# The last product of the position bias, one group of keys later

## The chip, the cores and the metric

The kernel runs on one NeuronCore of a Trainium2 chip. The time is the device time of one execution in microseconds; before the change it is 3762.87 us, the median of three runs (3762.15 to 3767.35). The profile is that of one more execution, with a span of 3758.9 us.

The engines have these names in it: PE is TensorE (matmul), PEld its weight load, DVE VectorE, ACT ScalarE, POOL GpSimd, SP SyncE.

## The reference

The network has four layers on x of shape (2, 512, 32, 32) in float32. The change is in layer 0, an attention with deformed keys: 8 heads and 2 images give 16 units (u in the kernel), each with 1024 queries and 64 keys. To each score a bias is added, that a small perceptron computes from the position of the query relative to the key:

```python
pos = grid_q[:, :, None, :] - grid_kv[:, None, :, :]
bias = jnp.sign(pos) * jnp.log1p(jnp.abs(pos))
bias = jax.nn.relu(bias @ cpb_w1 + cpb_b1)          # 2 -> 128
bias = jax.nn.relu(bias @ cpb_w2 + cpb_b2)          # 128 -> 128
bias = (bias @ cpb_w3 + cpb_b3).reshape(b, GROUPS, H * W, Hd * Wd)   # 128 -> 1
sim = jnp.einsum('bhid,bhjd->bhij', qh, kh) + bias
attn = jax.nn.softmax(sim, axis=-1)
```

That is done for 16 x 1024 x 64 pairs of query and key. The layer's own perceptron and layers 1 to 3 follow.

## The kernel before

A quad (u, o, jj) is a set of four keys of unit u; two of them (jj = 0 and 1) make a group (u, o), and there are 256 quads in 128 groups. For each quad VectorE makes the first hidden layer (line 390), one 128 x 1024 tile for each key. TensorE multiplies it with the second weights, 32 of the 128 outputs at a time (line 413). So there are four products q = 0 to 3 for a quad, each with the four keys side by side on the partitions. ScalarE applies the relu. The four results, each with its sign (flip), are added to one tile. Two of the three additions are made by transfers that add into their destination. The last of the three, `join`, is issued during the next quad, behind that quad's own first one.

```python
def second_hidden(self, u, o, jj, h1):
    nc = self.nc
    ys = []
    for q in range(4):
        hp = self.ps_h.tile([P, N], F32, tag="ps", ...)
        for h in range(2):
            cut = slice(h * HF, (h + 1) * HF)
            for k in range(4):
                rows = slice(32 * k, 32 * k + 32)
                nc.tensor.matmul(                                            # line 413
                    hp[rows, cut], lhsT=self.l0w2[:, 32 * q : 32 * q + 32], rhs=h1[k][:, cut], start=True, stop=True
                )
        y = self.hid2.tile([P, N], F32, tag=f"h2{q}", bufs=(2, 3, 2, 4)[q], ...)
        ys.append(y)
        nc.scalar.activation(y, hp, AF.Relu, bias=self.magb[:, q : q + 1])   # line 418
        if q == 1:
            nc.scalar.activation(ys[0], ys[0], AF.Copy, scale=self.flip[:, 0:1])               # line 420
            if jj == 1:
                nc.gpsimd.tensor_scalar(y, y, self.flip[:, 1:2], 1.0, ALU.mult, ALU.mult)      # line 422
            else:
                nc.scalar.activation(y, y, AF.Copy, scale=self.flip[:, 1:2])                   # line 424
            nc.gpsimd.dma_start(y, ys[0], accum_op=ALU.add)                  # line 425
            if self.join:
                self.join()
        elif q == 2:
            nc.gpsimd.tensor_scalar(y, y, self.flip[:, 2:3], 1.0, ALU.mult, ALU.mult)          # line 429
        elif q == 3:
            nc.gpsimd.tensor_tensor(y, y, ys[2], ALU.add)                    # line 431
    self.join = lambda: nc.gpsimd.dma_start(ys[3], ys[1], accum_op=ALU.add)  # line 432
    return ys[3]
```

The last product (line 445) multiplies the summed tiles z of the two quads of a group with one column per key, and so adds each key's bias to its row of the scores:

```python
def last_product(self, u, o, z, sims, ps_s):
    if o == 0:
        sims[u] = ps_s.tile([P, HF], F32, tag="sim", ...)      # one buffer
    for h in range(2):
        for jj in range(2):
            at = h * NJ + jj * 32
            nc.tensor.matmul(                                  # line 445
                sims[u][at : at + 32, :], lhsT=self.ends[:, 28 - 4 * o : 60 - 4 * o],
                rhs=z[jj][:, h * HF : (h + 1) * HF], start=(o == 0), stop=False,
            )
```

The loop over the quads has its order of instructions fixed for TensorE, ScalarE, VectorE and GpSimd. The first hidden layer is made one quad ahead. `offsets` and `sampled` (front: positions and sampled keys of the next pair of heads) and `attend` (after: the query-key product of line 460 on top of the bias, softmax, values) are cut into steps, and every quad takes one step of each.

```python
held, self.join = None, None
for i, (u, o, jj) in enumerate(quads):
    if o == 0 and jj == 0 and u % 2 == 0 and u // 2 + 1 < BP:
        nxt = pairs[u // 2 + 1]
        front += [self.offsets(nxt, ...), self.sampled(nxt, ...)]
    h1 = ready
    if i + 1 < len(quads):
        # (cut: before o = 7, front is driven on until the next pair's logarithms are there)
        ready = self.first_hidden(*quads[i + 1], pairs, tables)              # VectorE, line 390
    z = self.second_hidden(u, o, jj, h1)
    if jj == 0:
        first = z
    else:
        if held is not None:
            self.last_product(*held, sims, ps_s)
            if held[1] == 7:
                # (cut)
                after.append(self.attend(v, pairs[v // 2], sims.pop(v), att, ps))
        held = (u, o, (first, z))
    self.step(after)
    self.step(front)
self.join()
self.last_product(*held, sims, ps_s)
after.append(self.attend(u, pairs[u // 2], sims.pop(u), att, ps))
```

Of `offsets` the steps matter that put long work on VectorE: six products of a 6 x 6 window (line 243, three to a step) and their sum (line 256). Its first step sets the border of a padded tile to zero on GpSimd (line 232); that tile has two buffers, and `attend` reads the other pair's.

Of the kernel before, what the change touches and what calls it, by code (L numbers as in the profile page):

```python
# [11 lines left out]
F32 = mybir.dt.float32  # L12
AF = mybir.ActivationFunctionType
ALU = mybir.AluOpType
# [4 lines left out]
P = 128  # L19
B, C, H, W = 2, 512, 32, 32  # L20
N = H * W
# [5 lines left out]
BP = B * CT  # L27
# [20 lines left out]
class Net:  # L48
# [50 lines left out]
    def layer0(self):  # L99


        nc, io = self.nc, self.io
        with ExitStack() as ctx:
            keep = self.pool(ctx, "l0")
            self.l0qkv = keep.tile([P, 3, CT, P], F32, tag="qkv", name="qkv")
            nc.scalar.dma_start(self.l0qkv, io["l0_qkv"])
            self.l0w2 = keep.tile([P, P], F32, tag="w2", name="w2")
            nc.scalar.dma_start(self.l0w2, io["cpb_w2"])
            ow = keep.tile([P, CT, C], F32, tag="ow", name="ow")
            nc.scalar.dma_start(ow, io["out_w"])  # L110
            self.s1 = self.bn(keep, "bn1")
            self.last_weights(keep)

            self.dram = ctx.enter_context(self.tc.tile_pool(name="l0_d", bufs=2, space=bass.MemoryType.DRAM))
            self.fpool = self.pool(ctx, "f", 2)
            self.fone = self.pool(ctx, "f1", 1)
            self.lpool = self.pool(ctx, "c_log", 2)
            self.tab = self.pool(ctx, "c_tab", 2)
            self.hid = self.pool(ctx, "c_hid", 4)
            self.hid2 = self.pool(ctx, "c_hid2", 1)  # L120
            self.soft = self.pool(ctx, "c_soft", 1)
            apool = self.pool(ctx, "c_att", 1)
            ps = self.ps_h = self.pool(ctx, "c_ps_h", 3, psum=True)

            self.bank = self.pool(ctx, "c_ps_t", 1, psum=True).tile([P, HF], F32, tag="bank", name="bank")
            ps_s = self.pool(ctx, "c_ps_s", 1, psum=True)

            engines = {getattr(mybir.EngineType, e) for e in ("PE", "Activation", "DVE", "Pool")}
            with self.tc.manual_schedule(engines=engines):
                pairs = [{} for _ in range(BP)]  # L130
                for _ in self.offsets(pairs[0], 0, ps):
                    pass
                front = [self.sampled(pairs[0], 0, ps)]
                after, sims, att = [], {}, None
                tables = {}
                quads = [(u, o, jj) for u in range(2 * BP) for o in range(8) for jj in range(2)]
                ready = self.first_hidden(*quads[0], pairs, tables)
                held, self.join = None, None
                for i, (u, o, jj) in enumerate(quads):
                    if o == 0 and jj == 0 and u % 2 == 0 and u // 2 + 1 < BP:  # L140
                        nxt = pairs[u // 2 + 1]
                        front += [self.offsets(nxt, u // 2 + 1, ps), self.sampled(nxt, u // 2 + 1, ps)]
                    h1 = ready
                    if i + 1 < len(quads):
                        if quads[i + 1][1:] == (7, 0) and u + 1 < 2 * BP:
                            self.advance(front, lambda: "logs" in pairs[(u + 1) // 2])
                        ready = self.first_hidden(*quads[i + 1], pairs, tables)
                    z = self.second_hidden(u, o, jj, h1)
                    if jj == 0:
                        first = z  # L150
                    else:
                        if held is not None:
                            self.last_product(*held, sims, ps_s)
                            if held[1] == 7:
                                v = held[0]
                                if v % 8 == 0:
                                    self.advance(after, lambda: False)
                                    att = [
                                        apool.tile([P, N], F32, tag=f"att{t}", name=f"att{v}_{t}") for t in range(CT)
                                    ]  # L160
                                self.advance(front, lambda: "v" in pairs[v // 2])
                                after.append(self.attend(v, pairs[v // 2], sims.pop(v), att, ps))
                                if v % 8 == 7:
                                    after.append(self.projection(ps, att, ow, v // 8))
                        held = (u, o, (first, z))
                    self.step(after)
                    self.step(front)
                self.join()
                self.last_product(*held, sims, ps_s)
                after.append(self.attend(u, pairs[u // 2], sims.pop(u), att, ps))  # L170
                self.advance(after, lambda: False)
                self.project(ps, att, ow, "out_b", B - 1)
# [225 lines left out]
                h1.append(h[:, k, :, :].rearrange("p y x -> p (y x)"))  # L398
        return h1

    def second_hidden(self, u, o, jj, h1):

        nc = self.nc
        ys = []
        for q in range(4):
            hp = self.ps_h.tile([P, N], F32, tag="ps", name=f"hp_{u}_{o}{jj}{q}")
            for h in range(2):
# [3 lines that stand above are left out]
                    nc.tensor.matmul(  # L413
                        hp[rows, cut], lhsT=self.l0w2[:, 32 * q : 32 * q + 32], rhs=h1[k][:, cut], start=True, stop=True
                    )
            y = self.hid2.tile([P, N], F32, tag=f"h2{q}", bufs=(2, 3, 2, 4)[q], name=f"h2_{u}_{o}{jj}{q}")
            ys.append(y)
            nc.scalar.activation(y, hp, AF.Relu, bias=self.magb[:, q : q + 1])  # L418
            if q == 1:
                nc.scalar.activation(ys[0], ys[0], AF.Copy, scale=self.flip[:, 0:1])  # L420
                if jj == 1:
                    nc.gpsimd.tensor_scalar(y, y, self.flip[:, 1:2], 1.0, ALU.mult, ALU.mult)  # L422
                else:
                    nc.scalar.activation(y, y, AF.Copy, scale=self.flip[:, 1:2])  # L424
                nc.gpsimd.dma_start(y, ys[0], accum_op=ALU.add)  # L425
                if self.join:
                    self.join()
            elif q == 2:
                nc.gpsimd.tensor_scalar(y, y, self.flip[:, 2:3], 1.0, ALU.mult, ALU.mult)  # L429
            elif q == 3:  # L430
                nc.gpsimd.tensor_tensor(y, y, ys[2], ALU.add)  # L431
        self.join = lambda: nc.gpsimd.dma_start(ys[3], ys[1], accum_op=ALU.add)  # L432
        return ys[3]

    def last_product(self, u, o, z, sims, ps_s):
# [720 lines left out]
```

## Time and profile before

| | |
|---|---|
| Time, median of three runs | 3762.87 us |
| Layer 0 in the span | up to about 2260 us |
| Line 413, second hidden layer, TensorE | 1891.9 us in 16384 matmuls |
| Line 390, first hidden layer, VectorE | 1180.9 us in 1024 |
| Line 418, relu, ScalarE | 1120.3 us in 1024 |
| Line 431, addition, GpSimd | 614.8 us in 256, 2402 ns each |
| Line 429, sign, GpSimd | 448.8 us in 256 |
| Lines 425 and 432, adding transfers | 512 issues, 512 KB each, 6.5 us from issue to landing at the median |

A group of instructions on the page is given by line, engine and operation, with its busy time, the mean of one instruction, and the time for which its engine sat idle before it, with what ended that idle time. Two readings need care. A 32-column matmul of this kernel is listed with 593 ns, but four of them run side by side, so the listed times overlap. And a transfer's instruction on GpSimd covers only its issue; its end is the landing, which stands by itself. "Idle" of an engine that is not the bottleneck costs nothing.

### The profile page before, as it was taken

The numbers are of one execution on the slowest core, as the hardware profiler recorded it, in microseconds if no ns is written. First come the engines' busy times: TensorE is split into PE (matmuls) and PEld (weight loads), VectorE is DVE, ScalarE is ACT, GpSimd is POOL, SyncE is SP. The second block draws the span as 40 slices with busy tenths as digits, with TensorE's granted clock in tenths as the row PEclk, the third lists the DMA queues.
The fourth block names the chain that finished last, engine by engine and source line by source line (L and its number), as shares of the span: only waits on it lengthen the run. The fifth ranks groups of instructions, "written<-read, shape, count | busy, mean of one in ns | idle before, by whom it ended". The sixth has DMA issues, their size and how long they took to land.

```text
span 3758.9 us, 58788 instructions
## 1 busy us (share of the span) xinstructions
PE 3579.0 (95%) x25152; PEld 1393.5 (37%) x25152; DVE 2055.7 (55%) x2070; ACT 1972.0 (52%) x2001; POOL 1864.5 (50%) x1397
## 2 busy tenths in 40 slices
PE   5999999999999999999999989999989999999999
PEld 2333333333333333333333434444464333343333
DVE  5777766767766567767766641000052376522773
ACT  4776776777776576776777761000110266211661
POOL 3776776776776576776777760000001244012441
PEclk9999999999999999999999999999999999999999
DMA  5776776776776576776777762000000000000001
GB/s 143 142 139 135 142 147 126 148 143 133 142 150 127 113 146 123 145 147 129 158 145 148 153 139 114 0 0 0 0 3 0 34 1 1 16 0 1 1 1 46
DMA packets 102356, 336.77 MB, mean 90 GB/s; under 512 B 12608, under 2 KB 14272, under 8 KB 100800
## 3 DMA queue, kind: packets, MB, share of 16 engines
q0 software_dynamic: 73728, 268.47, 37.8%
q1 hardware_dynamic: 27488, 62.34, 5.5%
q8 instruction: 201, 3.29, 0.3%
q10 hardware_dynamic: 864, 2.06, 0.1%
q14 instruction: 75, 0.61, 0.1%
HBM read 59.92 MB, written 4.46 MB: 17 GB/s over the span
## 4 chain that ended last, share of the span: by engine, by line
PE 57%; POOL 15%; issue 12%; DMA 7%; DVE 6%; ACT 3%; POOLq 0%; ACTq 0%; SPq 0%; DVEq 0%
PE hp L413 15%; DMA h<-h 6%; POOL h L431 6%; PE m L549 6%; PE m L558 6%; PE s L886 6%; PE o L915 6%; PE pb L515 3%; PE qk0p L778 3%; PE qk1p L778 3%; POOL h L425 3%; PE vp L819 3%; POOL h L432 2%; ACT h L418 2%; DVE h L390 2%
## 5 line engine op out<-in xcount | busy, mean ns | idle before, releaser
L413 PE MATMUL hp<-h,w 128*32 128x512 f32 x16384 | 1891.9, 593 | 25.5 <-DVE h L390 18.1
L418 ACT ACTIVATE h<-hp,magb 128x1024 f32<-128x1024 f32 x1024 | 1120.3, 1111 | 586.3 <-PE hp L413 586.3
L390 DVE CUSTOM_DVE_ANT_1 h<-tx,bank 128x1024 f32<-128x1024 f32 x1024 | 1180.9, 1216 | 360.7 <-PE hp L413 352.3
L413 PEld LDWEIGHTS hp<-h,w 128*32 128x32 f32 x16384 | 668.8, 110 | 1130.6 <-issue 905.9
L431 POOL TENSOR_TENSOR h<-h,h 128x1024 f32<-128x1024 f32 x256 | 614.8, 2402 | 21.4
L425 POOL DMA_DIRECT2D h<-h x256 | 225.0, 879 | 547.6 <-ACT h L424 493.3
L429 POOL TENSOR_SCALAR h<-h,flip 128x1024 f32<-128x1024 f32 x256 | 448.8, 1753 | 0.0
L890 ACT ACTIVATE e<-s 128x1024 f32<-128x1024 f32 x256 | 258.6, 1023 | 152.9 <-PE s L886 152.7
L445 PE MATMUL sim<-h,ends 128*32 128x512 f32 x1024 | 229.2, 603 | 82.7 <-DMA h<-h 82.5
L432 POOL DMA_DIRECT2D h<-h x256 | 299.7, 1171 | 1.6 <-issue 1.3
L420 ACT ACTIVATE h<-h,flip 128x1024 f32<-128x1024 f32 x256 | 291.2, 1137 | 0.0
L886 PE MATMUL s<-q,k 64*64 64x512 f32 x2048 | 259.9, 590 | 5.4 <-ACT e L890 3.7
L915 PE MATMUL o<-e,v 64*64 64x512 f32 x2048 | 260.8, 592 | 0.0
L589 POOL MEMSET l1ones<- 128x128 f32 x1 | 0.2, 198 | 487.2 <-PE m L558 487.2
L549 PE MATMUL m<-mx,w 128*128 128x512 f32 x512 | 220.5, 592 | 0.9 <-issue 0.9
L553 ACT ACTIVATE mh<-m,cols 128x512 f32<-128x512 f32 x64 | 44.0, 687 | 336.5 <-PE m L549 336.5
L558 PE MATMUL m<-mh,w 128*128 128x512 f32 x512 | 220.4, 592 | 0.0
L897 POOL TENSOR_TENSOR some<-some,e 128x1024 f32<-128x1024 f32 x64 | 151.2, 2363 | 82.7 <-ACT e L890 80.3
L566 DVE SCALAR_TENSOR_TENSOR x<-m,cols,x 128x512 f32<-128x512 f32 x16 | 12.0, 751 | 318.0 <-PE m L558 318.0
L895 POOL TENSOR_TENSOR some<-e,e 128x1024 f32<-128x1024 f32 x32 | 75.7, 2367 | 212.9 <-ACT q L924 139.2
L792 POOL TENSOR_TENSOR sq<-q 128x1024 f32<-128x1024 f32 x16 | 30.3, 1893 | 280.1 <-DVE q L786 280.1
L422 POOL TENSOR_SCALAR h<-h,flip 128x1024 f32<-128x1024 f32 x128 | 152.3, 1190 | 30.6 <-ACT h L418 30.6
(184 smaller groups left out, 2796.2 us busy)
## 6 DMA issues: line engine op xcount, KB each, us to landing
h<-h POOLq DMA_DIRECT2D x512, 512.0 KB, 6.5
lb<-logs SPq DMA_DIRECT2D x64, 512.0 KB, 5.1
w<-in_mlp_w SPq DMA_DIRECT2D x8, 1024.0 KB, 11.9
qkv<-in_l_qkv SPq DMA_DIRECT2D x8, 768.0 KB, 6.5
x<-in_x SPq DMA_DIRECT2D x8, 512.0 KB, 7.9
out<-x SPq DMA_DIRECT2D x8, 512.0 KB, 2.6
proj<-in_l_proj SPq DMA_DIRECT2D x8, 256.0 KB, 5.9
l1w<-in_l_w SPq DMA_DIRECT2D x1, 1280.0 KB, 8.0
```

The source lines that it names most:

```text
L390: self.nc.vector._custom_dve(TENSOR_ADD_SAT, out=h[:, k, :, :], in0=x[:, jj, 2 * r + k, :].unsqueeze(1).to_broadcast([P, H, W]), in1=y[:, ...
L413: nc.tensor.matmul(hp[rows, cut], lhsT=self.l0w2[:, 32 * q : 32 * q + 32], rhs=h1[k][:, cut], start=True, stop=True)
L418: nc.scalar.activation(y, hp, AF.Relu, bias=self.magb[:, q : q + 1])
L420: nc.scalar.activation(ys[0], ys[0], AF.Copy, scale=self.flip[:, 0:1])
L425: nc.gpsimd.dma_start(y, ys[0], accum_op=ALU.add)
L429: nc.gpsimd.tensor_scalar(y, y, self.flip[:, 2:3], 1.0, ALU.mult, ALU.mult)
L431: nc.gpsimd.tensor_tensor(y, y, ys[2], ALU.add)
L432: self.join = lambda: nc.gpsimd.dma_start(ys[3], ys[1], accum_op=ALU.add)
L549: nc.tensor.matmul(acc, lhsT=w1[t][:, o * P : (o + 1) * P], rhs=xn[t], start=(t == 0), stop=(t == CT - 1))
L558: nc.tensor.matmul(acc, lhsT=w2[t // 4][:, t % 4, o * P : (o + 1) * P], rhs=hs[t], start=(t == 0), stop=(t == nh - 1),)
L886: nc.tensor.matmul(s[halves[c], par, :], lhsT=ks[p][rows, at : at + DH], rhs=qs[p][rows, cut], start=True, stop=True)
L915: nc.tensor.matmul(o[halves[par], r, :], lhsT=v[rows, n, at : at + DH], rhs=e[rows, par, :], start=(n == 0), stop=(n == NB - 1),)
```

## The change

The last product of a group is issued a quad later: behind the matmuls of the first quad (jj = 0) of the second group after it, where before it stood behind the second quad (jj = 1) of the first group after it. The adding transfer of the group's second quad so has one more quad of four keys in which to land. Up to two finished groups are held, and the tiles z get a fifth buffer. `attend`, which follows a unit's last product, moves along, and the front of the next pair of heads starts three quads later (o = 1, jj = 1), behind it. In the final quad the additions that were transfers, and the one of GpSimd, are made on VectorE, as nothing is left there to hide a transfer.

```diff
-                held, self.join = None, None
+                held, self.join = [], None
                 for i, (u, o, jj) in enumerate(quads):
-                    if o == 0 and jj == 0 and u % 2 == 0 and u // 2 + 1 < BP:
+                    if o == 1 and jj == 1 and u % 2 == 0 and u // 2 + 1 < BP:
...
-                    z = self.second_hidden(u, o, jj, h1)
-                    if jj == 0:
+                    z = self.second_hidden(u, o, jj, h1, i + 1 == len(quads))
+                    if jj == 1:
+                        held.append((u, o, (first, z)))
+                    else:
                         first = z
-                    else:
-                        if held is not None:
-                            self.last_product(*held, sims, ps_s)
-                            if held[1] == 7:
-                                v = held[0]
+                        if len(held) == 2:
+                            v, last, zs = held.pop(0)
+                            self.last_product(v, last, zs, sims, ps_s)
+                            if last == 7:
...
-                        held = (u, o, (first, z))
                     self.step(after)
                     self.step(front)
-                self.join()
-                self.last_product(*held, sims, ps_s)
+                self.join(True)
+                for done in held:
+                    self.last_product(*done, sims, ps_s)
...
-    def second_hidden(self, u, o, jj, h1):
+    def second_hidden(self, u, o, jj, h1, final):
+        def add(to, what, final=final):
+            if final:
+                nc.vector.tensor_tensor(to, to, what, ALU.add)
+            else:
+                nc.gpsimd.dma_start(to, what, accum_op=ALU.add)
...
-            y = self.hid2.tile([P, N], F32, tag=f"h2{q}", bufs=(2, 3, 2, 4)[q], name=f"h2_{u}_{o}{jj}{q}")
+            y = self.hid2.tile([P, N], F32, tag=f"h2{q}", bufs=(2, 3, 2, 5)[q], name=f"h2_{u}_{o}{jj}{q}")
...
-                nc.gpsimd.dma_start(y, ys[0], accum_op=ALU.add)
+                add(y, ys[0])
                 if self.join:
-                    self.join()
+                    self.join(final)
...
-                nc.gpsimd.tensor_tensor(y, y, ys[2], ALU.add)
-        self.join = lambda: nc.gpsimd.dma_start(ys[3], ys[1], accum_op=ALU.add)
+                (nc.vector if final else nc.gpsimd).tensor_tensor(y, y, ys[2], ALU.add)
+        self.join = lambda final: add(ys[3], ys[1], final)
```

## The prediction

> **What bounds the kernel now.** I read the page's busy line and slices first, then the chain of waits by line, then who waited for whom on TensorE and its weight loader, then the answers for lines 432 and 425 (the adding transfers), and last the order of time in a stretch with and one without a wait.
>
> ```profile
> PE 3579.0 (95%) x25152; PEld 1393.5 (37%) x25152; DVE 2055.7 (55%) x2070; ACT 1972.0 (52%) x2001; POOL 1864.5 (50%) x1397
> ...
> PE   5999999999999999999999989999989999999999
> ...
> DMA  5776776776776576776777762000000000000001
> ...
> L445 PE MATMUL sim<-h,ends 128*32 128x512 f32 x1024 | 229.2, 603 | 82.7 <-DMA h<-h 82.5
> ```
>
> TensorE is busy throughout, and layer 0 is the part with DMA digits of 5 to 7: some 2260 of 3759 us. The change touches nothing after it. Line 445, the last product of the bias, waits for the adding transfer. 82.5 us understates that, since the modelled ends of the matmuls run on into the wait. The weight loader shows it better:
>
> ```profile
> PEld sim L445 <- DMA h<-h: 164.4, 96, 6.7
> ...
> PEld hp L413 <- DVE h L390: 67.3, 71, 15.3
> ...
> PEld hp L413 <- ACT h L418: 30.9, 75, 1.3
> ```
>
> The columns are total us, times, longest. What a wait really costs is read from the period between two last products. Here are a group of keys without a wait (TensorE) and two with one (weight loader):
>
> ```profile
> 1068.32 1.04 PE L445 MATMUL sim<-h,ends 128*32 128x512 f32 x8
> 1069.17 13.92 PE L413 MATMUL hp<-h,w 128*32 128x512 f32 x128
> 1082.91 1.58 PE L445 MATMUL sim<-h,ends 128*32 128x512 f32 x5
> ```
> ```profile
> 2205.49 0.15 PEld L445 LDWEIGHTS sim<-h,ends 128*32 128x32 f32 x6 [2.43 <-DMA h<-h]
> ...
> 2222.06 0.15 PEld L445 LDWEIGHTS sim<-h,ends 128*32 128x32 f32 x6 [2.49 <-DMA h<-h]
> ...
> 2237.29 0.15 PEld L445 LDWEIGHTS sim<-h,ends 128*32 128x32 f32 x6 [1.14 <-DMA h<-h]
> 2244.09 0.18 PEld L445 LDWEIGHTS sim<-h,ends 128*32 128x32 f32 x2 [6.65 <-DMA h<-h]
> 2247.16 0.14 PEld L445 LDWEIGHTS sim<-h,ends 128*32 128x32 f32 x3 [2.89 <-DMA h<-h]
> ```
>
> Without a wait the period is 1082.91 - 1068.32 = 14.59 us: 128 matmuls of line 413 and 8 of line 445, at about 0.107 us each. With a wait of 2.49 it is 2222.06 - 2205.49 = 16.57. So a wait costs itself less about 0.5 us (2.49 - 1.98). The last three rows are the end of the layer: 6.65 and 2.89 us for a transfer that nothing can hide.
>
> Why it waits is in the answers for lines 432 and 425, in that order:
>
> ```profile
> DMA to landing us min/median/max: 4.6/7.1/10.0
> ```
> ```profile
> DMA to landing us min/median/max: 4.6/4.7/8.1
> ```
>
> The joining transfer (432) is issued right behind that of line 425. In the order of time of GpSimd, line 432 of a jj = 0 quad starts at 2230.70 where the quad's matmuls began at about 2222.5: 8.2 us into the group. It lands 7.1 us later at the median, at 15.3, when TensorE has been ready for the first half of the last product since 13.7. A landing at 10 would give 18.2.
>
> **What the Trainium skill says.** "DMA: Bandwidth & Descriptors", section "Issuing engines are not separate DMA queues": transfers issued by different engines run on the same 16 DMA engines and interleave. The trace agrees: page part 3 gives the adding queue 37.8% of 16 engines' span, 0.378 x 3759 / 512 = 2.8 us each, and 7.1 - 4.7 = 2.4 us is about one such transfer ahead. A table load (5.5%, 64 of them, 3.2 us each) ahead would explain the 10.0. "Perfetto Trace Analysis", section "DMA Instruction — SWDGE (GPSIMD)": the end shown on GpSimd is that of making the descriptors, not of moving the data. It agrees: line 432 shows 1.17 us and lands after 7.1. "GPSIMD Engine Reference", section "Elementwise — side-by-side cycle accounting": an fp32 add of two tensors is 1.96 times slower on GpSimd. The trace has 2402 ns (line 431) against 1225 ns for the same shape on VectorE (line 904): 1.96. "SBUF — State Buffer", section "Who interferes with whom": such an add on VectorE contends with a GpSimd instruction that reads SBUF. The adds moved here meet one GpSimd instruction at most; no run yet shows what it costs.
>
> **The change part by part.**
>
> *Later product.* No matmul, relu, add or transfer of the 127 earlier groups is removed. The last product of a group is issued behind the next jj = 0 quad instead of behind the jj = 1 quad before it: 64 matmuls x 0.107 = 6.9 us later. Ready time moves from 13.7 to 14.6 + 6.9 = 21.4 us into the group, against a landing at 15.3, or 18.2 at the worst. I expect every one of these waits to go. Their size: 164.4 us in 96 waits, less the three of the end (1.14 + 6.65 + 2.89 = 10.7) is 153.7 in 93; less 0.5 each gives 153.7 - 46.5 = 107 us.
>
> *What comes back on VectorE.* In the quads in which `offsets` puts three products of line 243 (3.7 us in the order of time) or the reduction of line 256 (4.45 us) before the hidden layer, VectorE has 4.6 + 3.7 us and more of work in a quad of 6.9 and TensorE already waits for line 390. Of its 67.3 us, 15 are the start. A wait of line 445 that lies beside such a quad only changes its name. In the stretch from 619 to 664 us those are the waits of 0.82 and 0.42; I take 1 to 2 us for each of 7 pairs: 12 us given back.
>
> *Front three quads later.* `offsets` begins behind `attend` and not before it. Line 232's memset on GpSimd waits 30.8 us in 6 times for line 460; that goes, but GpSimd has time to spare: its instructions of two quads follow each other in 12.6 us (per quad 0.59 + 0.58 for the transfers, 1.84, 2.37; 1.41 for line 422; 0.38 for half a table) of 14.59. I count 0.
>
> *One more buffer of h2, number 3.* Five tiles are live where four were; the slack for its reuse stays the same. 0.
>
> *The end.* Line 445 starts its last matmuls at 2247.16. On VectorE the chain is: flip of line 422 done at 2236.6, then four adds of 1.24 us without a transfer, done at about 2241.5. That saves 5.6 us. The last product but one then comes behind the final quad too, and its wait (as now, 1 to 2.5 us) lies under these adds.
>
> *What the faster pace brings.* The second hidden layer's tile h2, number 1, has three buffers and is read by the joining transfer: landing at 15.3 (18.2 with a table load ahead), needed again by the relu three quads on, 14.6 + 3.7 = 18.3 us into the same count. It fits with nothing over in the worst case. 5 us for that.
>
> Sum: 107 - 12 + 5.6 - 5 = 95 us, so 3763 - 95 = 3668 us, 2.5% less.
>
> **The rivals.**
>
> *GpSimd or the DMA engines become the bound.* For: the chain of waits runs through lines 431, 425 and 432 for most of the layer, and four adding transfers and half a table load take 4 x 2.8 + 1.6 = 12.7 of 14.59 us. Against: both fit, and GpSimd still idles for ScalarE's line 424 (493 us in 126 times, 3.9 us per group), more than the 2.0 us per group that a wait costs. The stretch at 1068 ran at 14.59 with GpSimd idle for 3.1 us. If landing times stretched so far that half the waits stayed, the time would be about 3715.
>
> *The wait moves to the buffers of h2, number 1.* Same mechanism, on ScalarE: relu waits for the landing. ScalarE waits for no transfer now. If the median landing rose to 10 us, some 0.5 us in half of the groups, 30 us: 3695.
>
> *VectorE takes it.* The shift places `attend`'s pieces beside other pieces of `offsets`. Per pair the overload sums to much the same in my count (about 9 us before and after), but if most waits beside the seven front stretches (some three per pair, 2 us each) came back as waits for line 390, 30 us more would be lost: 3700.
>
> *More than counted.* Waits for ScalarE (30.9) and part of those for VectorE may follow from the jolts of line 445; without them 20 us more: 3645.
>
> **Range and chances.** The 107 us are measured and their removal has 3 us of slack in the worst case, so slower is hardly possible. 2% is 75 us, that is 3688, and the deductions would have to grow by 20 us to miss it, which each of the first three rivals could do. I say 3640 to 3705, with 0.77 for faster by over 2%, 0.21 for within, 0.02 for slower.
>
> **What would show it.** Right: the weight loader's waits of line 445 for the transfer fall from 164 to under 10 us, last products in plain stretches come 14.6 us apart, and the waits for line 390 grow by 10 to 20 us; the landing of line 432 stays near 7.1 at the median; in the end no transfer stands between the final relu and line 445. Wrong: ScalarE's line 418 waiting for a transfer (the buffers), line 445 still waiting with landings over 13 us (the DMA engines), or line 413's waits for line 390 above 100 us (VectorE).

## The result and the profile after

The changed kernel takes 3600.47 us (median of four runs, 3599.09 to 3603.74), against 3765.11 us for the kernel before on the same chip. The ratio is 0.9564, with a 95% interval of 0.9547 to 0.958: 4.4% less, 165 us. The prediction said 95 us less and a range of 3640 to 3705 us. It had the direction right, and what makes the waits for the transfer go. The size of those waits and the worth of the later front it had wrong.

The page after, with the lines that answer to those shown before (line numbers have moved: 413 is now 422, 445 is 454, 390 is 391, 418 is 427, 460 is 469, 472 is 481; the adding transfers of lines 425 and 432 are both issued at 414):

```profile
PE 3500.6 (97%) x25152; PEld 1249.1 (35%) x25152; DVE 2019.9 (56%) x2074; ACT 1974.7 (55%) x2001; POOL 1871.8 (52%) x1393
...
PE 93%; DVE 5%; DMA 1%; issue 0%; ACT 0%; POOL 0%; ACTq 0%; SPq 0%; DVEq 0%; POOLq 0%
```

The second line is the chain that ended last, as shares of the span. In the kernel before it was:

```profile
PE 57%; POOL 15%; issue 12%; DMA 7%; DVE 6%; ACT 3%; POOLq 0%; ACTq 0%; SPq 0%; DVEq 0%
```

57% TensorE, 15% GpSimd and 7% transfers have become 93% TensorE. The loop from the last product through relu, sign, issue and landing back to the last product is cut.

The answer for the last product's line (columns of the waits: total us, times) and the order of time of TensorE near the end of the layer show the waits gone:

```profile
L454 PEld LDWEIGHTS sim<-h,ends x1024: 106/110/151, 81.4 to 2084.8; 128*32 128x32 f32 x171
...
  issue: 75.9, 254
  DVE h L412: 6.1, 3
  DMA h<-h: 0.9, 1
```
```profile
1951.87 1.04 PE L454 MATMUL sim<-h,ends 128*32 128x512 f32 x8
1952.73 13.92 PE L422 MATMUL hp<-h,w 128*32 128x512 f32 x128
1966.46 1.04 PE L454 MATMUL sim<-h,ends 128*32 128x512 f32 x8
```

164.4 us of waiting for the transfer in 96 waits have become 0.9 us in one, at the end of the layer. Two last products lie 1966.46 - 1951.87 = 14.59 us apart, the undisturbed period that the prediction read in the kernel before.

To see where all of the gain comes from, the weight loader's time in the loop of the quads is split by line. For each line, its busy time and the idle time just before it are added. Over all lines that makes up the whole stretch, but for loads of different lines that overlap (25.6 us of them before, 17.4 after). These are the two lines that matter, from the start of the first quad to the end of the last (42.1 to 2235.9 us before, 42.2 to 2079.0 after). First the kernel before, then the changed one:

```profile
L413 PEld LDWEIGHTS hp<-h,w 128*32 128x32 f32 x16384 | 668.8, 110 | 1130.6 <-issue 905.9 <-DVE h L390 67.3 <-ACT h L418 30.9
L445 PEld LDWEIGHTS sim<-h,ends 128*32 128x32 f32 x1009 | 44.5, 108 | 206.3 <-DMA h<-h 153.7 <-issue 44.4
```
```profile
L422 PEld LDWEIGHTS hp<-h,w 128*32 128x32 f32 x16384 | 528.9, 110 | 1242.3 <-issue 1152.5 <-DVE h L391 43.8 <-ACT h L427 28.5
L454 PEld LDWEIGHTS sim<-h,ends 128*32 128x32 f32 x1008 | 34.0, 110 | 75.3 <-issue 75.3
```

| Weight loader, busy and idle before, us | before | after | difference |
|---|---|---|---|
| Last product (445, 454) | 44.5 + 206.3 = 250.8 | 34.0 + 75.3 = 109.3 | -141.5 |
| Second hidden layer (413, 422) | 668.8 + 1130.6 = 1799.4 | 528.9 + 1242.3 = 1771.2 | -28.2 |
| Rest of the stretch (all other lines, less the overlap) | 143.5 | 156.2 | +12.7 |
| Stretch | 2193.7 | 2036.7 | -157.0 |

The sums are safer than the parts: the second hidden layer has 140 us less busy time after and 112 us more idle time. With each instant of the stretch counted only once, the three differences are -140.8, -23.6 and +7.4 us. The end of the layer gives another 5 us: from the last matmul of the second hidden layer to the transposes for softmax it was 2251.48 - 2235.8 = 15.6 us and is 2089.36 - 2078.9 = 10.4. Together that is the 162 us by which the two profiled executions differ (spans of 3758.9 and 3597.3).

So the waits were worth 141 us and not 107. And the second hidden layer did not give back 12 us to VectorE but got 28 us faster: the loader's waits for line 390 fell from 67.3 to 43.8 us. The prediction's sum had nothing of the kind (only its rival "more than counted" allowed 20 us for such waits), and three explanations were open: the later start of the front takes these waits away by itself; or they vanish as a consequence of the other waits; or the front is worth much more and the waits for the transfer really only 107 us.

### The profile page after: what moved, and what is told of

The parts are those of the page before. It is cut to its first block, busy times and chain, and to the rows that moved or that the text cites. A ratio compares the mean times of both kernels' runs of the same rounds, so it can differ in the third digit from the quotient of the medians.

```text
span 3597.3 us, 58774 instructions
## 1 busy us (share of the span) xinstructions
PE 3500.6 (97%) x25152; PEld 1249.1 (35%) x25152; DVE 2019.9 (56%) x2074; ACT 1974.7 (55%) x2001; POOL 1871.8 (52%) x1393
## 3 DMA queue, kind: packets, MB, share of 16 engines
q0 software_dynamic: 73296, 266.90, 39.2%
## 4 chain that ended last, share of the span: by engine, by line
PE 93%; DVE 5%; DMA 1%; issue 0%; ACT 0%; POOL 0%; ACTq 0%; SPq 0%; DVEq 0%; POOLq 0%
PE hp L422 47%; PE m L558 6%; PE m L567 6%; PE o L924 6%; PE s L895 6%; PE pb L524 3%; PE qk0p L787 3%; PE qk1p L787 3%; PE sim L454 3%; PE vp L828 3%; PE out_b L524 2%; DVE h L391 2%; DVE prod L244 1%; PE d L941 1%; DVE conv L257 1%
## 5 line engine op out<-in xcount | busy, mean ns | idle before, releaser
L422 PE MATMUL hp<-h,w 128*32 128x512 f32 x16384 | 1823.4, 593 | 17.7 <-DVE h L391 16.2
L422 PEld LDWEIGHTS hp<-h,w 128*32 128x32 f32 x16384 | 528.9, 110 | 1242.3 <-issue 1152.5
L414 POOL DMA_DIRECT2D h<-h x509 | 452.3, 1026 | 377.1 <-ACT h L433 319.9
L899 ACT ACTIVATE e<-s 128x1024 f32<-128x1024 f32 x256 | 258.6, 1024 | 153.4 <-PE s L895 153.3
L429 ACT ACTIVATE h<-h,flip 128x1024 f32<-128x1024 f32 x256 | 291.3, 1138 | 0.0
L799 ACT ACTIVATE k<-qk1p,cols 128x512 f32<-128x512 f32 x32 | 22.0, 688 | 243.5 <-PE qk1p L787 243.5
L433 ACT ACTIVATE h<-h,flip 128x1024 f32<-128x1024 f32 x128 | 145.6, 1138 | 0.0
```

The costliest lines, as they stand in the source:

```text
L414: nc.gpsimd.dma_start(to, what, accum_op=ALU.add)
L422: nc.tensor.matmul(hp[rows, cut], lhsT=self.l0w2[:, 32 * q : 32 * q + 32], rhs=h1[k][:, cut], start=True, stop=True)
L899: nc.scalar.activation(e, s, AF.Exp)
```

## The experiments

All ratios are to the kernel before, run on the same chip within the same set of runs. Its own median differs by up to 0.2% from set to set, so ratios are compared and not times.

**The front later, alone.**

```diff
-                    if o == 0 and jj == 0 and u % 2 == 0 and u // 2 + 1 < BP:
+                    if o == 1 and jj == 1 and u % 2 == 0 and u // 2 + 1 < BP:
```

> The kernel before, with only the front of the next pair of heads started three quads later (o = 1, jj = 1). Theory A (two separate gains: the waits of line 445 for the transfer are worth about 140 us, and the later front takes about 20 us of waits for VectorE's line 390 away): 3745 us, with the weight loader's waits for line 390 down from 67 to about 44 us and those for the transfer still near 160. Theory B (the waits for the transfer are worth the predicted 107 us, the rest of the gain is the later front's): 3715 us. Theory C (the waits for line 390 fell only because those of line 445 did): 3763 us, no change.

Measured: ratio 0.9988 (0.9979 to 0.9997), 5 us. The loader in the loop of the quads:

```profile
L413 PEld LDWEIGHTS hp<-h,w 128*32 128x32 f32 x16384 | 675.0, 110 | 1106.0 <-issue 892.3 <-DVE h L390 56.6 <-ACT h L418 32.6
L445 PEld LDWEIGHTS sim<-h,ends 128*32 128x32 f32 x1009 | 45.7, 109 | 214.2 <-DMA h<-h 163.8 <-issue 41.7
```

The second hidden layer is indeed faster, 1799.4 - (675.0 + 1106.0) = 18 us, but the last product waits longer for the transfer (163.8 against 153.7 us) and takes 9 us more, and the rest of the stretch 7 us. Theory A had named the 20 us and had them arrive in the time, which they did not; B is far off. C's time is right, but not its reason, since the second hidden layer does change.

**No wait for the join, everything else as before.** The joining transfer moves the same bytes into spare tiles; its share of the sum is left out of the output.

```diff
+            self.spare = [keep.tile([P, N], F32, tag=f"spare{k}", name=f"spare{k}") for k in range(3)]
...
-        self.join = lambda: nc.gpsimd.dma_start(ys[3], ys[1], accum_op=ALU.add)
+        self.turn += 1
+        aside = self.spare[self.turn % 3]
+        self.join = lambda: nc.gpsimd.dma_start(aside, ys[1], accum_op=ALU.add)
```

> The kernel before, with the joining transfer of line 432 adding into one of three spare tiles and not into z, so that as many bytes move but the last product waits for no transfer; a quarter of the bias's sum is so left out, and the output is not the reference's. The front stays early. Theory A: the waits' full worth and a few us at the end, 3763 - 141 - 3 = about 3620 us, with waits for line 390 still near 65 us. Theory B: about 3655 us. Theory C: waits for line 390 fall to about 44 us as well, about 3600 us.

Measured: ratio 0.9655 (0.964 to 0.967), 3637 us.

```profile
L417 PEld LDWEIGHTS hp<-h,w 128*32 128x32 f32 x16384 | 534.6, 110 | 1281.2 <-issue 1144.8 <-DVE h L394 73.4 <-ACT h L422 53.4
L451 PEld LDWEIGHTS sim<-h,ends 128*32 128x32 f32 x1008 | 35.2, 110 | 75.5 <-issue 73.4 <-POOL h L426 1.2 <-POOL tx L370 0.3
```

The last product falls to 110.7 us, by 140.1: this is what the waits cost in that line, in the old order and without any other part of the change, and it agrees with the 141.5 us of the changed kernel. But the second hidden layer rises to 1815.8, by 16.4 us, with waits for VectorE up to 73.4 and for ScalarE from 30.9 to 53.4. That is the give-back that was predicted at 12 us. It exists, so long as the front is early. Group by group it lies beside the front: in 18 groups the loader waits more than 1.2 us for VectorE in either kernel; their 17.6 us of waits for the transfer went, and together they still became 1.8 us longer. A is right on the waits; the time was 17 us above its figure, and it had left out the give-back. C is out, as the waits for VectorE did not fall.

**Both.**

> The kernel before with both: the join set aside into spare tiles (its share of the sum left out) and the front three quads later. If the two effects simply add, 3637 - 5 = 3632 us. If they are coupled (a later front takes VectorE's waits away, but so long as line 445 waits for a transfer whose landing follows from the pace of the quads, that time only goes into longer waits there), the second hidden layer's time falls as from the run with the join aside to the changed kernel, some 37 us, and the time is 3600 us within 5, with waits for line 390 near 44 us on the weight loader.

The edit is the two diffs above together. Measured: ratio 0.9592 (0.9577 to 0.9607). With the waits standing, the later front is worth 0.1%; with the waits gone, 0.6% (0.9655 to 0.9592). The four runs in one table, as the stretch of the quads, from the first weight load to the last:

| Stretch of the quads, us | front early | front late |
|---|---|---|
| waits for the join | 2193.7 | 2191.8 |
| join aside | 2073.8 | 2046.3 |

The effects don't add: 1.9 us in the first row, 27.5 in the second. The profiled execution with both was the fastest of its four (3609.89 us, median 3616.85), so 27.5 is high; the ratios give about 5 and 24 us. The longer waits of the first run fit this reading: while line 445 waits for a landing, the moment of that landing follows from when the group began, and a quad made faster only reaches the wait earlier. The expected 37 us were not all there, though, nor did the waits for VectorE come down to 44:

```profile
PEld hp L417 <- DVE h L394: 55.5, 51, 16.1
```

The changed kernel has 43.8 here and a stretch of 2036.7. What remains between the two, some 10 us, goes with the last product, and `attend` behind it, standing a quad later; no run separates that further.

**How much later is late enough.** The changed kernel with the last product behind the first of the four products of the jj = 0 quad.

```diff
             nc.scalar.activation(y, hp, AF.Relu, bias=self.magb[:, q : q + 1])
+            if q == 0 and early is not None:
+                early()
```

(`early` issues the last product of the group that is due; in the loop it is taken from `held` before the quad and not after it.)

> The changed kernel, with the last product behind the first of the four products (q = 0) of the jj = 0 quad and not behind its fourth: ready 1.7 us after the end of the group and not 6.9. Landing theory (the joining transfer lands at 15.3 us into the group at the median and up to 18.2 with a table load ahead; ready time here 14.6 + 1.7 = 16.3): waits come back in the groups with a table load ahead only, some 20 to 60 waits of 1 to 2 us, 30 to 60 us slower than the changed kernel, 3630 to 3660 us. Rival (landings follow the pace and a small delay is enough): under 10 us of waits, 3600 us.

Measured: ratio 0.965 (0.9635 to 0.9664), 3634 us, inside the expected range.

```profile
L459 PEld LDWEIGHTS sim<-h,ends x1024: 105/110/152, 75.2 to 2117.7; 128*32 128x32 f32 x171
...
  DMA h<-h: 27.7, 44
```

That answer adds TensorE's and the loader's waits; the loader's alone are 25.9 us in 40. They come back in about a third of the groups and are 0.65 us each, where 1 to 2 us had been expected. The table load is not all of it: 25 of the 40 awaited transfers had one in flight beside them, 15 had none. So a delay of 1.7 us takes most of the waits away and not all, as a landing spread around 15 to 18 us into the group would have it.

**The end of the layer.**

```diff
-                    z = self.second_hidden(u, o, jj, h1, i + 1 == len(quads))
+                    z = self.second_hidden(u, o, jj, h1, False)
...
-                self.join(True)
+                self.join(False)
```

> The changed kernel, with the additions of the final quad made by transfers and GpSimd again. Expected: the end costs 5.2 us more (from the last matmul of the second hidden layer to the transposes of line 472: 15.6 us in the profile before, 10.4 after), so 3606 us. Rival: the end was hidden or shifted elsewhere, no difference within 1 us.

Measured: 3605.73 us, ratio 0.9573 (0.9559 to 0.9586). The difference to 3600.47 is what was expected, but the two ratios' intervals overlap, so it is the trace that carries this reading:

```profile
PEld sim L454 <- DMA h<-h: 9.7, 3, 6.6
```

The three waits of the end are back, the longest 6.6 us as in the kernel before.

**Can the rest of the waits for VectorE go?** Two edits of the changed kernel, alone and together. Finer steps:

```diff
-            if ky % 3 == 2:
+            if ky % 2 == 1:
                 yield
...
-        nc.vector.tensor_reduce(conv, prod.rearrange("p a b j -> p j (a b)"), AX.X, ALU.add)
-        yield
+        for cut in (slice(0, NJ // 2), slice(NJ // 2, NJ)):
+            nc.vector.tensor_reduce(conv[:, cut], prod[:, :, :, cut].rearrange("p a b j -> p j (a b)"), AX.X, ALU.add)
+            yield
```

> The changed kernel with offsets cut finer: two of the six window products to a step where there were three, and the sum of line 257 in two halves, one to a step. The weight loader still waits 43.8 - 15 = 29 us for line 391 because single steps put 4 to 5 us of VectorE work before the hidden layer. Theory: the load of a quad falls under the 2 us of slack or near it, most of the 29 us go, 3580 us. Rival: what counts is not the size of a step but that it stands behind a VectorE instruction that waits for TensorE (the transposes of attend); then under 10 us, 3595 us.

Measured: ratio 0.9603 (0.959 to 0.9616), slower than the changed kernel by 0.4%. Neither theory had that. The loader shows why:

```profile
PEld hp L423 <- DVE h L392: 40.6, 37, 15.8
PEld bank L333 <- DVE h L392: 27.0, 7, 5.3
```

The waits of the second hidden layer are hardly less, and a new one has come: the product of `sampled` (line 333) waits 27 us in 7 times behind VectorE. Two more steps for `offsets` move `sampled` by two quads, and what it multiplies, made by VectorE, now comes late. Besides, 12 of the 48 window products took over 1.95 us each, against 6 in the changed kernel; what slows them is told with the next run.

The order of the two steps at a quad's end:

```diff
-                    self.step(after)
-                    self.step(front)
+                    self.step(front)
+                    self.step(after)
```

> The changed kernel with the two calls at the end of a quad exchanged: the step of the front is issued before the step of attend, so that the window products do not stand behind VectorE's wait for attend's transposes. If the order behind that wait is what makes TensorE wait, 10 to 20 us faster, 3585 us; if only the sum of work in a quad counts, 3600 us.

Measured: ratio 0.9462 (0.9449 to 0.9475), more than the 10 to 20 us expected.

```profile
L422 PEld LDWEIGHTS hp<-h,w 128*32 128x32 f32 x16384 | 526.8, 110 | 1223.8 <-issue 1160.5 <-ACT h L427 27.3 <-DVE h L391 18.2
```

15.4 of these 18.2 us are the start, so nearly all other waits for VectorE are gone. What the order does is seen on VectorE. First the changed kernel, then this one:

```profile
605.61 0.69 DVE L501 COPY pt<-pp 128x512 f32<-128x512 f32 x1 [3.70 <-PE pp L497]
606.22 5.28 DVE L244 TENSOR_TENSOR prod<-qpad,cols 128x384 f32<-128x384 f32 x3
611.43 0.47 DVE L379 TENSOR_SCALAR bank<-lb,cols 128x256 f32<-128x256 f32 x1
612.03 4.62 DVE L391 CUSTOM_DVE_ANT_1 h<-tx,bank 128x1024 f32<-128x1024 f32 x4
```
```profile
594.62 2.59 DVE L244 TENSOR_TENSOR prod<-qpad,cols 128x384 f32<-128x384 f32 x3
598.40 0.69 DVE L501 COPY pt<-pp 128x512 f32<-128x512 f32 x1 [1.20 <-PE pp L497]
599.01 0.48 DVE L379 TENSOR_SCALAR bank<-lb,cols 128x256 f32<-128x256 f32 x1
599.62 4.62 DVE L391 CUSTOM_DVE_ANT_1 h<-tx,bank 128x1024 f32<-128x1024 f32 x4
```

In the first, VectorE stands idle for 3.70 us for a transpose that TensorE makes at the end of the quad, and only then takes up the three window products, with the next hidden layer behind them. In the second the products fill idle time ahead of the transpose. But there is a second difference: the three products take 5.28 us in the first and 2.59 in the second. In the first, an addition runs on GpSimd beside them (from the order of time of GpSimd), and behind them the weight loader waits for VectorE three times, 2.76 us in all:

```profile
607.28 2.77 POOL L440 TENSOR_TENSOR h<-h,h 128x1024 f32<-128x1024 f32 x1
```
```profile
614.43 0.14 PEld L422 LDWEIGHTS hp<-h,w 128*32 128x32 f32 x2 [0.78 <-DVE h L391]
...
615.56 0.14 PEld L422 LDWEIGHTS hp<-h,w 128*32 128x32 f32 x2 [0.99 <-DVE h L391]
...
616.69 0.16 PEld L422 LDWEIGHTS hp<-h,w 128*32 128x32 f32 x8 [0.99 <-DVE h L391]
```

Over the whole run, the answers for the window products (ns: min, median, max) are these, changed kernel first:

```profile
L244 DVE TENSOR_TENSOR prod<-qpad,cols x48: 822/880/2926, 17.9 to 1647.7; 128x384 f32<-128x384 f32 x48
```
```profile
L244 DVE TENSOR_TENSOR prod<-qpad,cols x48: 822/881/1634, 17.8 to 1615.8; 128x384 f32<-128x384 f32 x48
```

All 48 together take 62.4 us in the changed kernel and 49.6 in this one. All six that took over 1.95 us there ran beside a GpSimd addition; here none took so long. So the exchange does two things: it puts the products into idle time, and it moves them off GpSimd's additions. The 2.69 us by which the three products differ would be nearly all of the 2.76 us of waits. No run separates the two.

> Both together. If each takes away the same 29 us of waits, 3577 us at best, which is no better than the better of the two by more than 5 us; if attend's instructions now come late behind the front's, some waits of TensorE for attend's softmax appear and it is 3590 us.

Measured: ratio 0.9464 (0.9451 to 0.9477), no different from the order alone. Finer steps gain nothing more.

**Is it the order or the sharing of quads?** The join aside, the front early, with the steps exchanged.

> The kernel before with the join set aside (its share of the sum left out), the front still early (o = 0, jj = 0), but the front's step issued before attend's in every quad. If TensorE's waits for line 390 come from window products that stand behind VectorE's wait for attend's transposes, the order alone takes them away: loader waits for line 390 from 73 to 25 us or less, and 3637 - 35 = about 3600 us. If they come from the front's and attend's work falling into the same quads, whatever the order, they stay at 60 to 73 us and the time at 3630 us.

Measured: ratio 0.9602 (0.9587 to 0.9616), against 0.9655 with the old order.

```profile
PEld hp L417 <- DVE h L394: 52.8, 44, 15.1
```

The waits fall from 73.4 to 52.8 us, between the two expectations and nearer the second. Less the 15 us of the start: 58 with the front early and behind `attend`, 38 early and first, 40 late and behind, all three with the join aside. In the changed kernel it is 29 with the front behind and 3 with the front first. Order and placement each take a part, and it needs both. The additions on GpSimd have a share here too: 16 window products took over 1.95 us in this run, against 12 with the join aside and the old order, and all 48 together 76.1 us against 69.9. They do not explain the placement, as with the late front it is 12 products and 69.8 us again.

**The better version beside the changed kernel.**

> The changed kernel unaltered, beside the next one on the same chip: ratio to the kernel before 0.956, with which the next is compared.

> The changed kernel with the front's step before attend's, again: ratio 0.946; if the difference to the changed kernel was one of the chip or the day, it shrinks to nothing here, otherwise it is about 1% (30 to 38 us).

Measured: 0.9551 (0.9538 to 0.9564) and 0.9469 (0.9456 to 0.9482); 3600.08 and 3568.79 us on the same chip. The exchanged steps are 31 us faster than the change as it stands, and this is the best version found: 5.3% less than the kernel before.

## Why the prediction was wrong

By its own steps, with what each term measured:

| Term of the sum | predicted, us | measured, us |
|---|---|---|
| Waits of line 445 | -107 | -141.5 |
| Second hidden layer (give-back on VectorE, front later) | +12 | -28.2 |
| Rest of the stretch | 0 | +12.7 |
| Buffers of h2, number 1 | +5 | 0 |
| End | -5.6 | -5.2 |
| Sum | -95 | -162 |

- *Later product, what removes the wait:* right. Ready time against landing, 21.4 us against 15.3 to 18.2, left no wait in the loop, and the run with 16.3 left some. The longest landing of the changed kernel took 11.1 us where it had been 10.0, which by the same count gives 19.3, still ahead of 21.4.
- *Later product, the size:* wrong, by 34 us. The failing step is to apply "So a wait costs itself less about 0.5 us" to all 93 waits. With the join aside, 153.7 us of waits went and the last product took 140.1 us less: 13.6 / 93 = 0.15 us per wait on average. The 14.59 us hold, though the group from which they were read did end in a wait, of 0.83 us, just behind its second time stamp. The 0.5 us were no misreading either: the two groups from which they came each follow a group that waited too. Set group by group against the run with the join aside, the 41 groups of that kind (next to no other work on TensorE, a wait in the group before) are longer by their wait less 0.51 us at the median. In 37 others that waited, the group is longer by the wait and 0.13 us more at the median. The rest are the 18 beside the front and 30 that waited 0.3 us or less. Both kinds stand in the weight loader's order of time:

```profile
488.39 0.13 PEld L445 LDWEIGHTS sim<-h,ends 128*32 128x32 f32 x4 [0.30 <-issue]
...
505.34 0.15 PEld L445 LDWEIGHTS sim<-h,ends 128*32 128x32 f32 x6 [2.24 <-DMA h<-h]
...
537.23 0.15 PEld L445 LDWEIGHTS sim<-h,ends 128*32 128x32 f32 x6 [0.71 <-DMA h<-h]
...
552.45 0.15 PEld L445 LDWEIGHTS sim<-h,ends 128*32 128x32 f32 x6 [1.14 <-DMA h<-h]
```

The first wait of 2.24 us follows a group without one: 505.34 - 488.39 = 16.95 us, 2.36 more than 14.59. The last, of 1.14 us, follows a wait: 552.45 - 537.23 = 15.22, only 0.63 more.
- *What comes back on VectorE:* the mechanism is there: 16 us with the front early, against 12 (21 with each instant counted once). As a part of this change it is wrong, because of the next step.
- *Front three quads later, "I count 0":* wrong. The count looked at GpSimd, where the wait for line 460 did go, and at the sum of VectorE's work per quad, which I found the same before and after. It did not look at the order in VectorE's queue, where window products stand behind an instruction that waits for TensorE, nor at how long these products take beside GpSimd's additions. With the join aside, the later start brought the stretch down by 27.5 us (24 by the ratios). That it does so is shown; how much of it is the order in the queue is not.
- *Buffers of h2, number 1:* the rival did not appear. ScalarE waits for no adding transfer in the changed kernel.
- *GpSimd or the DMA engines as the bound:* did not appear. The median from issue to landing of all adding transfers is 6.5 us as before, and GpSimd still idles 319.9 us for ScalarE's sign (493.3 before).
- *The end:* right, though not in its detail. The flip of the third product on GpSimd took 2.38 us beside the two adds on VectorE, where its mean is 1.75:

```profile
2078.96 2.36 DVE L412 TENSOR_TENSOR h<-h,h 128x1024 f32<-128x1024 f32 x2 [8.94 <-POOL h L431]
2082.26 1.23 DVE L440 TENSOR_TENSOR h<-h,h 128x1024 f32<-128x1024 f32 x1 [0.94 <-POOL h L438]
```

VectorE then waited 0.94 us for it. That fits what the Trainium skill says in "SBUF — State Buffer", section "Who interferes with whom": such an add contends with a GpSimd instruction that reads SBUF. The prediction said that no run yet showed the cost of such a meeting. The kernel before did, in its window products, which read two tensors as these adds do:

```profile
L243 DVE TENSOR_TENSOR prod<-qpad,cols x48: 821/889/2967, 17.6 to 1746.4; 128x384 f32<-128x384 f32 x48
```

- *Range:* the rival "more than counted" was given 20 us. Its reason did not hold: with the join aside, the waits for ScalarE and VectorE grew. All others pointed to slower, so the range was lopsided around a sum whose largest term had been read from two groups.

## What to carry to other kernels

A wait's cost is to be read from all its instances, by adding up busy and idle time by line over the stretch, and not from the period of one or two, which can be right and yet not stand for the others. A loop that ends on a transfer's landing hides what other changes are worth: the later front gave 2 to 5 us while the loop stood and 24 to 27 once it was cut, so such changes should be tried again afterwards. And in an engine's queue, try to put work that is free of dependencies ahead of an instruction that waits for another engine; exchanging two calls gave 31 us here. Look then at what the moved work meets on other engines, as part of the gain may be that.

## What was not expected of the hardware

The adding transfers hardly slowed down at the faster pace: their queue went from 37.8% to 39.2% of the 16 engines' span, the median landing stayed at 6.5 us, and only the longest rose, from 10.0 to 11.1 us. An estimated 12.7 us of transfers in each group of 14.59 had looked close to a bound, and no other sign of one was seen.

The window products on VectorE (128 x 384, 0.82 to 0.92 us with nothing on GpSimd beside them) were held up by additions that they share no tile with. In the traces of all 13 runs, 155 of them began while GpSimd ran a 128 x 1024 addition, and each ended 0.64 to 0.71 us after that addition did.
